# A graph-attention kernel of four layers on four streams: another order of the steps, and another agenda for their preparation

## The chip, the cores and the metric

The kernel runs on one core of a Trainium2 chip. The metric is the device time of one execution in microseconds (us). TensorE (PE in the profile) does matrix products and transposes, VectorE (DVE), ScalarE (ACT) and GpSimd (POOL) do elementwise work, SyncE (SP) starts the DMA transfers. Each engine has its own queue of instructions and waits for the others through semaphores.

## The reference, cut to what matters

There are 16 batch items of 1024 nodes with 256 features, one adjacency matrix for all, and four layers. Each layer normalises, clips at zero, and adds an attention layer to the residual `x`:

```python
h = jnp.maximum(_layernorm(x, axis=-1), 0.0)
x = x + _Ln_gnn_ref(h, adj, W, a)

# one attention layer (layers 0 and 2: four heads of 64; layers 1 and 3: one head of 256)
Wh = h @ W
e = leaky(e_src[:, None] + e_dst[None, :])        # 1024 x 1024 for each head
e = where(adj > 0, e, -big)
out = elu(softmax(e, axis=-1) @ Wh)               # relu in layer 3
```

The kernel does one layer of one item in a *step*; there are 16 x 4 = 64 steps, with four items ("streams") in flight. All is float32.

## The kernel before: the parts that the change touches

A step has three parts. Its **preparation**: statistics of `x`, normalisation, transposes, projection to `whx` (the projected features, with a column of weights), and the row factors `g`, which are sent through DRAM to all partitions. Its **weights and aggregation**: VectorE makes a tile `w` of 128 x 1024 attention weights for each head and each of eight column blocks, TensorE multiplies it with `whx`, ScalarE evicts the result to `y`. Its **finish**: divide by the sum of weights, ELU, add to `x`.

```python
# preparation (pieces in the order of the agenda)
def stats(half):            # 2 pieces; VectorE, four chunks each
    for c in range(half * HALF, (half + 1) * HALF):
        nc.vector.bn_stats(bn[:, c, :], xs[b][:, c, :])
    ...                     # after half 1: combine, ten small operations on GpSimd -> rstd, shift
def normalise(half):        # 2 pieces; ScalarE, four chunks each
        nc.scalar.activation(xn[:, q, :], xs[b][:, c, :], AF.Identity,
                             bias=st["shift"][:, c:c + 1], scale=st["rstd"][:, c:c + 1])
def transpose(half, k):     # TensorE, four transposes; then ScalarE evicts with Relu
def project(c):             # TensorE, two matmuls; then ScalarE (and GpSimd for four heads)
out = [stats(0), stats(1), normalise(0), normalise(1)]
for half in range(2):
    out += [transpose(half, 0), transpose(half, 1)]
    out += [project(c) for c in the half's four chunks]
out += [factors, rows, fetch_heads(n + 1), None]       # 20 pieces in all

# finish: (slot of the following step, piece)
def scaled(half):           # GpSimd: y times 1/sum; then min(y, 0)
def exponential(half):      # ScalarE
def add(half):
    nc.vector.scalar_tensor_tensor(e, e, -1.0, yh, op0=ALU.add, op1=ALU.max)
    nc.gpsimd.tensor_add(xh, xh, e)
return [(0, divide), (0, scaled(0)), (1, scaled(1)), (1, exponential(0)), (2, exponential(1)),
        (2, add(0)), (3, add(1))] + ...                # layer 3: another add, then store, load

# the main loop: every step has eight groups, "slots" k = 0..7
for n in range(len(steps)):
    for k, (h, i0, per) in enumerate(groups(n)):
        ...
        emit_tiles(place[n, h, C - 1] + 1, must=True)   # weights that this group needs
        aggregate(n, h, i0, per)                        # TensorE, then eviction on ScalarE
        if i0 + per == C:
            done["free"] = place[n, h, C - 1] + 1
        while ending and ending[0][0] <= k:             # finish of step n - 1
            ending.pop(0)[1]()
        ...
        prepare(8 * n + k)                              # pieces of the agenda that are due
        ahead = 6 if per > 1 else 3
        emit_tiles(min(done["tiles"] + ahead, done["free"] + WBUFS))   # weights ahead; WBUFS = 18
    ...
    ending = finish(n)
```

Everything is emitted in this order, and each engine does its instructions in the order of emission. Weights for a step are made ahead only once its preparation is complete by the agenda. A step with four heads has two groups for each head, with 64 aggregation matmuls of 64 output rows in each; a step with one head has eight groups of eight matmuls of 128 rows. (The profile counts each float32 matmul twice.)

The **agenda** says for each of the 20 pieces of step n's preparation in which slot it is emitted, counted in slots of the whole program from `8 * (n - 2)`. Before the change:

```python
AFTER_FOUR = (-3, -2, -1, 0, 1, 1, 2, 2, 3, 3, 4, 4, 5, 5, 6, 6, 7, 8, 8, 10)
SOON = (0, 0, 1, 2, 3, 3, 4, 4, 5, 5, 5, 5, 6, 6, 7, 7, 8, 9, 9, 11)
AFTER_ONE = (0, 1, 2, 3, 4, 4, 5, 5, 6, 6, 7, 7, 8, 8, 9, 9, 10, 11, 11, 13)
LATE = (0, 0, 1, 1, 2, 2, 3, 3, 3, 3, 3, 3, 4, 4, 4, 4, 5, 6, 6, 8)

for n, (b, l) in enumerate(steps):
    free = 8 * (last[b % STREAMS] + 1) + (8 if l == 0 else 5) if b % STREAMS in last else -99
    ...
    if free > start + kind[0]:          # the stream's step before isn't finished by then
        kind = LATE
        start = max(free, agenda_of[-1][0] + 5)
    agenda_of.append([start + k for k in kind] if n > 1 else ...)
```

`last` is the step in which the same stream was last worked on. In the order before, a stream's steps are four apart in most of the program (three to six at its ends), and the numbers of heads of the steps run 4 1 4 1 4 1 1 4 1 4 4 1 4 1 1 4 and so on: pairs of steps with four heads and pairs with one head occur.

Of the kernel before, what the change touches and what calls it, by code (L numbers as in the profile page):

```python
# [35 lines left out]
STREAMS = 4  # L36
# [2 lines left out]

AFTER_FOUR = (-3, -2, -1, 0, 1, 1, 2, 2, 3, 3, 4, 4, 5, 5, 6, 6, 7, 8, 8, 10)
SOON = (0, 0, 1, 2, 3, 3, 4, 4, 5, 5, 5, 5, 6, 6, 7, 7, 8, 9, 9, 11)
AFTER_ONE = (0, 1, 2, 3, 4, 4, 5, 5, 6, 6, 7, 7, 8, 8, 9, 9, 10, 11, 11, 13)
LATE = (0, 0, 1, 1, 2, 2, 3, 3, 3, 3, 3, 3, 4, 4, 4, 4, 5, 6, 6, 8)


LAYERS = [
    (4, 0.2, 0, 0),  # L50
    (1, 0.2, 0, 0),
    (4, 0.2, 128, 1),
    (1, 0.01, 0, 1),
]
# [3 lines left out]
def kernel(ctx: ExitStack, tc: tile.TileContext, x, adj, ws, avs, out):  # L58
# [38 lines left out]

    L = len(LAYERS)
    steps = order_of_steps(B, L)
    xs = {}  # L100
    state = [dict() for _ in steps]
# [337 lines left out]
    last, agenda_of = {}, []  # L439
    for n, (b, l) in enumerate(steps):  # L440

        free = 8 * (last[b % STREAMS] + 1) + (8 if l == 0 else 5) if b % STREAMS in last else -99
        last[b % STREAMS] = n
        start = 8 * (n - 2)
        before = [LAYERS[steps[max(n - i, 0)][1]][0] for i in (0, 1, 2)]
        if before[2] == 1:
            kind = SOON if before[:2] == [4, 1] else AFTER_ONE
        else:
            kind = SOON if l == 0 else AFTER_FOUR
        if free > start + kind[0]:  # L450
            kind = LATE
            start = max(free, agenda_of[-1][0] + 5)
        agenda_of.append([start + k for k in kind] if n > 1 else [-2] * 10 + [-1] * 10)
        if n > 2:

            was = agenda_of[n - 1]
            assert agenda_of[n][2] >= was[4] and agenda_of[n][3] >= was[10]
# [95 lines left out]
def order_of_steps(B, L):  # L553


    depth = B // STREAMS * L
    one = [[(k // L * STREAMS + s, k % L) for k in range(depth)] for s in range(STREAMS)]
    turns = [0, 1, 2, 0, 3, 2] + [0, 1, 2, 3] * (depth - 4) + [1, 0, 3, 2, 1, 0, 3, 2, 1, 3]
    return [one[s].pop(0) for s in turns]


# [22 lines left out]
```

## Time and profile before

| | before |
|---|---|
| median of 3 runs | 2699.22 us (2696.39 to 2703.35) |
| span of the profiled run | 2700.4 us |
| mean granted clock of TensorE | 0.984 |
| the chain that ended last, by engine | PE 82%, DVE 8%, ACT 4%, issue 3%, POOL 2%, DMA 1% |
| the chain, costliest lines | aggregation 61%, projection 17%, weight tiles 6%, transposes 4% |
| one weight tile on VectorE, 1280 of them | 1274 ns |
| DMA engines, mean rate over the span | 48 GB/s |

A line of instruction groups reads: line of the kernel, engine, operation, what is written and read, shapes, count, then the busy time in us with the mean of one in ns, then the idle time of that engine just before them with what ended it. A line of the timeline reads: start in us, length in us, engine, line, operation, tiles, shapes, count, and in brackets the engine's idle time before it and what released it. In a table of stretches each row gives the stretch, its length, the busy time of each engine with the number of instructions, the granted clock, the DMA share and GB/s.

### The profile page before, as it was taken

Reading aid. Unit: us, or ns where it says so; the run is one execution under the profiler, and the core shown is the slowest. Engines: PE = TensorE matmul, PEld = TensorE weight load, DVE = VectorE, ACT = ScalarE, POOL = GpSimd, SP = SyncE. Lnnn points to the kernel's source line nnn. Section 1 sums busy time; section 2 is a strip of 40 time slices with the busy share of each in tenths; the row PEclk is TensorE's granted clock in tenths of the full one; section 3 lists DMA queues with packets and bytes.
Section 4 is the critical chain, followed back from the end, with each engine's and each line's share of the span. In section 5 each row is a group of like instructions: output and inputs, shape, how many; then the busy total and the mean of one; then the engine's idle time right before and its main releaser. Section 6 shows DMA issues by size and latency. Waiting matters only on the chain.

```text
span 2700.4 us, 89532 instructions
## 1 busy us (share of the span) xinstructions
PE 2567.4 (95%) x40080; PEld 2271.1 (84%) x40080; DVE 1903.4 (70%) x2059; ACT 1228.1 (45%) x3338; POOL 987.8 (37%) x1234
## 2 busy tenths in 40 slices
PE   4899999999999999999999999999999999999998
PEld 3787888888888888888888888888888888788876
DVE  5796586477785688667875778748687567678742
ACT  4343445445444544554444554544435444444431
POOL 2143433532514434344242353452342443443321
PEclk8899999999999999999999999999999999999999
DMA  4211101112012111002211201101202110111011
GB/s 137 76 42 37 30 26 41 35 62 81 26 61 67 42 42 33 18 33 72 73 34 49 72 33 43 41 25 57 80 27 72 63 41 19 34 40 43 33 33 55
DMA packets 63694, 130.12 MB, mean 48 GB/s; under 512 B 6224, under 2 KB 41808, under 8 KB 63312
## 3 DMA queue, kind: packets, MB, share of 16 engines
q1 hardware_dynamic: 61984, 123.88, 13.7%
q8 instruction: 316, 5.18, 0.8%
q10 hardware_dynamic: 1328, 0.52, 0.1%
q14 instruction: 66, 0.54, 0.1%
HBM read 106.95 MB, written 17.43 MB: 46 GB/s over the span
## 4 chain that ended last, share of the span: by engine, by line
PE 82%; DVE 8%; ACT 4%; issue 3%; POOL 2%; DMA 1%; DVEq 0%; SPq 0%; ACTq 0%; POOLq 0%
PE acc L327 61%; PE pp L255 17%; DVE w L311 6%; PE pp L243 4%; DVE bn L205 1%; ACT xn L235 1%; DMA wx<-in_L_gnn_W 1%; POOL rstd L226 1%; ACT whx L257 1%; ACT g L306 0%; ACT e L361 0%; ACT whx L261 0%; PE pp L282 0%; ACT y L331 0%; POOL y L352 0%
## 5 line engine op out<-in xcount | busy, mean ns | idle before, releaser
L327 PE MATMUL acc<-whx,w 128*64 128x65 f32 x36864 | 1951.8, 242 | 41.3 <-DVE w L311 30.4
L327 PEld LDWEIGHTS acc<-whx,w 128*64 128x64 f32 x36864 | 1768.0, 146 | 223.5 <-issue 69.9
L311 DVE SCALAR_TENSOR_TENSOR w<-g,rcol,mask 128x1024 f32<-128x1024 f32 x1280 | 1544.1, 1274 | 440.5 <-ACT g L306 394.6
L331 ACT ACTIVATE y<-acc 128x260 f32<-128x260 f32 (+1 forms) x512 | 196.5, 384 | 1089.8 <-PE acc L327 1089.7
L255 PE MATMUL pp<-wx,hT 128*128 128x258 f32 (+1 forms) x2048 | 514.1, 394 | 5.7 <-ACT hT L244 3.2
L352 POOL TENSOR_TENSOR y<-y,r 128x1024 f32<-128x1024 f32 x128 | 242.3, 1897 | 618.0 <-DVE r L348 614.4
L255 PEld LDWEIGHTS pp<-wx,hT 128*128 128x128 f32 x2048 | 376.2, 191 | 75.1 <-ACT whx L261 6.0
L266 POOL TENSOR_TENSOR whx<-whx 128x256 f32<-128x256 f32 x256 | 160.0, 629 | 461.5 <-ACT whx L264 460.4
L368 POOL TENSOR_TENSOR x<-x,e 128x1024 f32<-128x1024 f32 x96 | 226.6, 2365 | 274.7 <-DVE e L367 250.1
L235 ACT ACTIVATE xn<-x,shift,rstd 128x256 f32<-128x256 f32 x512 | 264.2, 590 | 135.0 <-POOL shift L229 122.4
L367 DVE SCALAR_TENSOR_TENSOR e<-e,y 128x1024 f32<-128x1024 f32 x96 | 117.7, 1226 | 197.1 <-ACT e L361 197.1
L257 ACT ACTIVATE whx<-pp,nbias 128x4 f32<-128x4 f32 (+1 forms) x512 | 134.9, 264 | 166.4 <-PE pp L255 155.2
L243 PE MATMUL pp<-ident,xn 128*128 128x128 f32 x1024 | 158.7, 288 | 43.7 <-ACT xn L235 34.1
L205 DVE BATCH_NORM_STATS2 bn<-x 128x6 f32<-128x256 f32 x512 | 173.0, 407 | 28.5 <-DMA x<-in_x 25.8
L243 PEld LDWEIGHTS pp<-ident,xn 128*128 128x128 f32 x1024 | 117.1, 144 | 82.5 <-ACT xn L235 43.8
L306 ACT ACTIVATE g<-gs 128x1024 f32<-128x1024 f32 x160 | 162.4, 1018 | 8.4 <-DVE w L311 5.4
L244 ACT ACTIVATE hT<-pp 128x512 f32<-128x512 f32 x256 | 142.9, 592 | 26.6 <-PE pp L243 24.5
L261 ACT ACTIVATE whx<-pp,whx 128x256 f32<-128x256 f32 x256 | 121.4, 474 | 0.0
L220 POOL TENSOR_TENSOR dev<-bn 128x8 f32<-128x8 f32 x63 | 16.1, 256 | 276.5 <-DVE bn L205 276.5
L361 ACT ACTIVATE e<-e 128x1024 f32<-128x1024 f32 x96 | 100.8, 1050 | 30.0 <-POOL e L357 30.0
L226 POOL TENSOR_TENSOR rstd<-rstd,neghalf 128x8 f32<-128x8 f32 (+1 forms) x65 | 107.0, 1646 | 19.2 <-DVE shift L227 14.3
L357 POOL TENSOR_SCALAR e<-y 128x1024 f32<-128x1024 f32 x96 | 99.8, 1040 | 8.4
(58 smaller groups left out, 550.7 us busy)
## 6 DMA issues: line engine op xcount, KB each, us to landing
gs<-grow SPq DMA_DIRECT2D x160, 512.0 KB
out<-x SPq DMA_DIRECT2D x32, 512.0 KB
x<-in_x SPq DMA_DIRECT2D x15, 1024.0 KB
w<-in_adj SPq DMA_DIRECT2D x8, 512.0 KB
x<-in_x SPq DMA_DIRECT2D x2, 512.0 KB
wx<-in_L_gnn_W SPq DMA_DIRECT2D x3, 256.0 KB
e<-in_L_gnn_a SPq DMA_DIRECT2D x6, 128.0 KB
grow<-gT SPq DMA_DIRECT2D x32, 16.0 KB
```

The costliest lines, as they stand in the source:

```text
L205: nc.vector.bn_stats(bn[:, c, :], xs[b][:, c, :])
L235: nc.scalar.activation(xn[:, q, :], xs[b][:, c, :], AF.Identity, bias=st["shift"][:, c:c + 1], scale=st["rstd"][:, c:c + 1])
L243: nc.tensor.transpose(pt[:, q, :], st["xn", half][:, q, k * P:(k + 1) * P], ident)
L255: nc.tensor.matmul(pw, lhsT=st["hT", half][:, k, q * P:(q + 1) * P], rhs=wx[l][:, k, :], start=(k == 0), stop=(k == K - 1))
L257: nc.scalar.activation(whx[:, c, :, D], pw[:, F + H:F + 2 * H], AF.Exp, bias=nbias[l], scale=slope)
L266: nc.gpsimd.tensor_tensor(whx[:, c, :, 0:D], whx[:, c, :, 0:D], whx[:, c, :, D:D + 1].to_broadcast([P, H, D]), op=ALU.mult)
L306: nc.scalar.activation(g, state[n]["gs", h], AF.Copy)
L311: nc.vector.scalar_tensor_tensor(w, state[n]["g", h], state[n]["rcol"][:, jc, h:h + 1], masks[LAYERS[steps[n][1]][3]][:, jc, :], op0=ALU.m ...
L327: nc.tensor.matmul(acc[o % P:o % P + cols, q, :], lhsT=st["w", h, jc][:, o:o + cols], rhs=st["whx"][:, jc, h, :], start=(jc == 0), stop=(j ...
L331: nc.scalar.activation(st["y"][:, i0:i0 + per, h, :], acc, AF.Copy)
L352: nc.gpsimd.tensor_tensor(yh, yh, r[:, :, None].to_broadcast([P, HALF * H, D]), op=ALU.mult)
L368: nc.gpsimd.tensor_add(xh, xh, e)
```

## The change

The steps are put into another order, in which a step with four heads and a step with one head alternate strictly in all but the first and last few. A stream's step with one head then comes three steps after its last one, its step with four heads five after. The agenda follows: one list for steps with four heads (the former `AFTER_FOUR`), a new one for those with one head, and `SOON` only for the first steps. The earliest slot for a preparation after the finish of the stream's last step moves from 5 to 2. What is computed, the instructions and the buffers stay as they are. The aim is an even load: a step with four heads needs 32 weight tiles from VectorE, one with a single head 8, so that VectorE can make tiles for the first while the second is aggregated.

```diff
-AFTER_FOUR = (-3, -2, -1, 0, 1, 1, 2, 2, 3, 3, 4, 4, 5, 5, 6, 6, 7, 8, 8, 10)
+FOUR = (-3, -2, -1, 0, 1, 1, 2, 2, 3, 3, 4, 4, 5, 5, 6, 6, 7, 8, 8, 10)
+ONE = (2, 3, 4, 5, 5, 5, 6, 6, 7, 7, 7, 7, 8, 8, 8, 8, 9, 10, 10, 12)
 SOON = (0, 0, 1, 2, 3, 3, 4, 4, 5, 5, 5, 5, 6, 6, 7, 7, 8, 9, 9, 11)
-AFTER_ONE = (0, 1, 2, 3, 4, 4, 5, 5, 6, 6, 7, 7, 8, 8, 9, 9, 10, 11, 11, 13)
 LATE = (0, 0, 1, 1, 2, 2, 3, 3, 3, 3, 3, 3, 4, 4, 4, 4, 5, 6, 6, 8)
...
-        free = 8 * (last[b % STREAMS] + 1) + (8 if l == 0 else 5) if b % STREAMS in last else -99
+        free = 8 * (last[b % STREAMS] + 1) + (8 if l == 0 else 2) if b % STREAMS in last else -99
...
-        before = [LAYERS[steps[max(n - i, 0)][1]][0] for i in (0, 1, 2)]
-        if before[2] == 1:
-            kind = SOON if before[:2] == [4, 1] else AFTER_ONE
-        else:
-            kind = SOON if l == 0 else AFTER_FOUR
+        kind = ONE if LAYERS[l][0] == 1 else SOON if n < 4 else FOUR
...
     depth = B // STREAMS * L
     one = [[(k // L * STREAMS + s, k % L) for k in range(depth)] for s in range(STREAMS)]
-    turns = [0, 1, 2, 0, 3, 2] + [0, 1, 2, 3] * (depth - 4) + [1, 0, 3, 2, 1, 0, 3, 2, 1, 3]
+    turns = [0, 1, 2, 0, 3, 1, 2] + [0, 3, 1, 0, 2, 1, 3, 2] * (depth // 2 - 2)
+    turns += [0, 3, 1, 0, 2, 3, 1, 2, 3]
```

## The prediction

> **What bounds the kernel now.** I read the page first, then the groups by form, then stretches of the span cut at the ends of steps, then the timeline around one step. I call a step of a layer with four heads a *four-step*, one with a single head a *one-step*, and the eight parts into which the schedule cuts every step its *slots* 0 to 7.
>
> The page's busy line and its slices:
>
> ```profile
> PE 2567.4 (95%) x40080; PEld 2271.1 (84%) x40080; DVE 1903.4 (70%) x2059; ACT 1228.1 (45%) x3338; POOL 987.8 (37%) x1234
> ...
> PE   4899999999999999999999999999999999999998
> ```
>
> TensorE is busy 95% of the span and short of that only at the ends. The table of stretches says how much is left to win (columns: us, then busy us of PE, PEld, DVE, ACT, POOL, then the granted clock):
>
> ```profile
> 74.00:480.30 406.30, 377.39 (x6980) 336.59 (x6977) 310.80 (x342) 177.14 (x472) 143.06 (x182) 0.96 0.13 42
> 480.30:2208.20 1727.90, 1695.83 (x26420) 1506.96 (x26420) 1242.07 (x1323) 813.24 (x2226) 659.40 (x814) 1.00 0.15 49
> 2208.20:2700.00 491.80, 462.22 (x6514) 403.17 (x6513) 314.91 (x328) 203.11 (x551) 167.32 (x196) 0.98 0.12 38
> ```
>
> In the 43 steps of the middle stretch TensorE is idle 1727.9 - 1695.8 = 32 us, at the two ends 29 and 30 us. Step by step (cut at the last eviction of each) the middle idle lies in four-steps, above all where two of them are neighbours: one-steps last 32.5 to 35.7 us with next to no idle time, four-steps alone 44.4 to 48 us with 0.1 to 2.3 us, and the second of a pair looks like this:
>
> ```profile
> 1319.80:1366.40 46.60, 42.10 (x1053) 38.30 (x1048) 44.48 (x45) 18.27 (x47) 17.69 (x22) 0.96 0.05 14
> ```
>
> There VectorE is busy 44.5 of 46.6 us and TensorE waits for it. That is what strict alternation is meant to cure.
>
> [...] here the residual add takes 2.36 us on GpSimd and the two-input step before it 1.23 us on VectorE. [...] after the idle of 4.43 us shown below, the stretch
>
> ```profile
> 2328.20:2331.40 3.20, 3.03 (x30) 2.41 (x32) 1.94 (x4) 3.20 (x8) 2.43 (x6) 0.50 0.00 0
> ```
>
> has a granted clock of 0.50.
>
> **The change, part by part.** No instruction is added or removed; all durations of single instructions stay. Three things move.
>
> *Order.* I wrote out both sequences. Before, a stream's steps are mostly four apart and pairs of four-steps and of one-steps occur twice in 16 steps. After, from step 7 to 59, every four-step is followed by a one-step; a four-step comes five after its stream's last, a one-step only three. For 25 of the one-steps (numbers 10 to 58) the picture is the same: its predecessor is four-step M-1, its preparation falls into one-step M and the next four-step, and it runs as M+2.
>
> *Gain.* With no pairs, TensorE's idle time in the middle should nearly vanish: of the 32 us I count 25. [...] seconds of pairs have a mean clock of 0.96, so 0.04 x 46 = 1.8 us each for five of them, 9 us. For the ends I count 20 of the 59 us: the old order has seven steps there that come three after their predecessor, some with long waits; what the new order has of that kind is counted below. And some 9 us from smaller gaps on the weight-load side, which is my guess. Sum: -63 us.
>
> *Cost.* In M the finish of M-1 and the preparation of M+2 now meet. The finish adds the halves of the residual in slots 2 and 3; the new agenda puts the statistics of half 0 in slot 2, of half 1 in slot 3, right behind them, the normalisation of half 0 in slot 4 and its transposes on TensorE in slot 5. (The release moved from 5 to 2 allows it; before it was the statistics in slot 5 at the earliest.) What these steps take in a one-step after a four-step can be read in the kernel before, from step 54, which began at 2295. It is the timeline, with lines of other work left out:
>
> ```profile
> 2303.46 1.23 DVE L367 SCALAR_TENSOR_TENSOR e<-e,y 128x1024 f32<-128x1024 f32 x1 [6.93 <-ACT e L361]
> 2304.77 2.35 POOL L368 TENSOR_TENSOR x<-x,e 128x1024 f32<-128x1024 f32 x1 [2.14 <-DVE e L367]
> ...
> 2307.86 3.67 DVE L311 SCALAR_TENSOR_TENSOR w<-g,rcol,mask 128x1024 f32<-128x1024 f32 x3 [3.17 <-ACT g L306]
> ...
> 2311.44 1.22 DVE L367 SCALAR_TENSOR_TENSOR e<-e,y 128x1024 f32<-128x1024 f32 x1
> ...
> 2312.73 2.35 POOL L368 TENSOR_TENSOR x<-x,e 128x1024 f32<-128x1024 f32 x1 [5.62 <-DVE e L367]
> 2316.02 0.39 ACT L331 ACTIVATE y<-acc 128x257 f32<-128x257 f32 x1 [3.09 <-PE acc L327]
> ...
> 2322.51 0.21 POOL L220 TENSOR_TENSOR dev<-bn 128x8 f32<-128x8 f32 x1 [7.42 <-DVE bn L205]
> ...
> 2326.72 4.04 ACT L235 ACTIVATE xn<-x,shift,rstd 128x256 f32<-128x256 f32 x8 [6.84 <-POOL shift L229]
> ...
> 2327.37 0.33 PE L243 MATMUL pp<-ident,xn 128*128 128x128 f32 x1 [4.43 <-ACT xn L235]
> ```
>
> Now put the changed preparation into these times. The first add on GpSimd ends at 2304.77 + 2.35 = 2307.1. VectorE, waiting for it, makes four statistics (0.34 each, as 1.40 for four elsewhere in this timeline): 2308.5. The three weight tiles of slot 2 (3.67; their row factors are there by 2307.8): 2312.2. The second exponential step (1.22): 2313.4. The second add (2.35, and 0.1 of handover): 2315.9. Four statistics: 2317.3. The ten small GpSimd operations, here 2322.51 to 2326.72, 4.2 us: 2321.5. The first of the normalised blocks (0.6): 2322.2. TensorE meanwhile: slot 5's aggregation ends where its eviction begins, at 2316.0, and the transposes are next in its queue. So it stands idle 2322.2 - 2316.0 = 6.2 us. Then the transposes follow at the pace of the normalisation: in step 54 they took 2327.37 to 2330.10, 2.7 us, against 1.1 for eight undisturbed ones (1.09 in other parts of the trace): 1.6 us. Then the half clock. Step 3 of the kernel before shows it whole:
>
> ```profile
> 256.96 2.80 PE L243 MATMUL pp<-ident,xn 128*128 128x128 f32 x8 [5.66 <-ACT xn L235]
> 259.69 5.48 PE L327 MATMUL acc<-whx,w 128*64 128x65 f32 x128
> ```
>
> A group of 128 of these takes 3.95 us elsewhere, so 1.5 us more; [...] I count 1.3. Sum for one step: 6.2 + 1.6 + 1.3 = 9.1 us, nothing of it beside other TensorE work, since TensorE is what was full. Times 25: 228 us. The four projections that slot 0 of the next four-step now takes in one go cost little: 16 matmuls in a row took 4.01 us before, as much as two times eight at 2.01; I count 0.3 each, 7 us for 25.
>
> *Sum.* 2700 - 63 + 228 + 7 = 2872 us, said as 2870.
>
> **The rivals.** (1) *The alternation wins clean.* VectorE has its idle time in one-steps (10 to 20 of 34 us), the schedule seems made for them, and a statistic that waits there costs VectorE nothing. Then the gain of 63 us is all: about 2637 us. Against it speaks that not VectorE's time but the length of a chain counts: from the first exponential step to the first transpose 18.7 us are needed (2303.46 to 2322.2), and TensorE's slot 5 is over 12.5 us after that start (2316.0). (2) *Half of it.* If the three weight tiles don't get between the two exponential steps, because their row factors come late or in another order, the chain is 3.7 us shorter: 2.5 us idle, 1.6 of pace, and no half clock[...]: 4.1 x 25 = 103 us, so 2700 - 63 + 103 + 7 = 2747 us. For it: in some steps of before the two stand next to each other. Against it: the agenda marks the four-step's preparation as complete in slot 2, ahead of the tiles there. (3) *VectorE becomes the bound of the four-steps.* It needs some 30 tiles of 1.274 us (the mean of the weight group) plus two exponential steps of 1.2, 41 us, against TensorE's 45: close, but the ten tiles that the buffers allow ahead are made in the one-step. If it fails, 2 us per pair, 50 us more: 2920.
>
> **Range and chances.** Rival 2 and mixtures with the main case give the lower part, rival 3 and longer half clocks the upper: 2770 to 2925 us. The cost of a stall would have to fall below (63 - 7)/25 = 2.2 us for a faster kernel at all, and to nothing for more than 2% (below 2645): 0.05. Within 2% (up to 2753) means (2753 - 2700 + 56)/25 = 4.4 us at most: 0.07, as rival 2 lies just there. Slower: 0.88.
>
> **What would show it.** Right: TensorE's transposes with idle time before them of some 6 us, 25 times, released by the normalisation; ScalarE's normalisation released by GpSimd's shift; one-steps of some 43 us where before they were 34, four-steps at 45 to 46 without VectorE filling them; TensorE's busy share down to about 90% and a granted clock near 0.96. Wrong: transposes that wait under 1 us; or four-steps that grow instead; or, if the chain is there but short, the second exponential step directly behind the first half's statistics.

## The result, and the profile after

The changed kernel takes 2911.39 us (median of 4 runs, 2911.21 to 2912.41) against 2699.3 us before: a ratio of 1.0785, 95% interval 1.0767 to 1.0804. It is slower by 212 us; 2870 us were predicted, with a range of 2770 to 2925.

The page of the changed kernel, the busy line, the slices of TensorE and of its clock:

```profile
PE 2640.7 (91%) x40080; PEld 2292.7 (79%) x40080; DVE 1907.4 (66%) x2059; ACT 1232.6 (42%) x3338; POOL 975.5 (34%) x1234
...
PE   4889999999999999999999999999999999999988
...
PEclk8999999999999999999999999999999999999999
```

The busy share of TensorE fell by four points, and the slices still show nines: a loss of some 8% in short pieces hides in slices of 73 us. The table of stretches, cut at the ends of steps 8 and 58 (steps are counted from 0; after the busy times the granted clock), shows where it lies:

```profile
0.00:483.50 483.50, 401.77 (x6221) 348.38 (x6222) 328.88 (x400) 204.75 (x540) 164.18 (x234) 0.93 0.16 54
483.50:2700.00 2216.50, 2056.11 (x31298) 1784.47 (x31298) 1460.16 (x1543) 960.57 (x2622) 764.70 (x950) 0.96 0.13 43
2700.00:2909.60 209.60, 182.83 (x2570) 159.90 (x2566) 118.35 (x118) 67.30 (x177) 46.67 (x50) 0.93 0.12 39
```

The kernel before, cut at the ends of the same steps, in the same view:

```profile
0.00:480.30 480.30, 409.33 (x7148) 360.97 (x7149) 346.42 (x411) 211.77 (x563) 161.05 (x224) 0.95 0.17 55
480.30:2507.60 2027.30, 1981.84 (x31252) 1758.71 (x31252) 1461.53 (x1553) 951.14 (x2602) 780.13 (x960) 0.99 0.14 47
2507.60:2700.40 192.80, 176.21 (x1683) 151.43 (x1681) 95.44 (x98) 65.21 (x175) 46.59 (x50) 0.96 0.12 42
```

The middle grew by 2216.5 - 2027.3 = 189 us: TensorE's idle time from 45 to 160 us, its busy time by 74 us with the same matmuls, at a mean clock of 0.96 in place of 0.99. The start grew by 3 us, the end by 209.6 - 192.8 = 17 us. (The ends don't hold the same work, as the counts of matmuls show: the new order has five four-steps among its first nine steps and two among its last five, the old one six and one.) What the middle's idle time waits for (the view of waits, for TensorE in this stretch; us in total, times, longest):

```profile
PE pp L242 <- ACT xn L234: 146.2, 24, 6.1
```

The transposes wait for the normalisation, once in each pair of steps. One of these, in the timeline of the changed kernel, a one-step that began at 1154:

```profile
1162.30 1.22 DVE L366 SCALAR_TENSOR_TENSOR e<-e,y 128x1024 f32<-128x1024 f32 x1 [7.84 <-ACT e L360]
1163.61 2.35 POOL L367 TENSOR_TENSOR x<-x,e 128x1024 f32<-128x1024 f32 x1 [3.05 <-DVE e L366]
...
1165.99 1.40 DVE L204 BATCH_NORM_STATS2 bn<-x 128x6 f32<-128x256 f32 x4 [2.47 <-POOL x L367]
1167.31 3.65 DVE L310 SCALAR_TENSOR_TENSOR w<-g,rcol,mask 128x1024 f32<-128x1024 f32 x3
...
1170.88 1.21 DVE L366 SCALAR_TENSOR_TENSOR e<-e,y 128x1024 f32<-128x1024 f32 x1
...
1172.17 2.35 POOL L367 TENSOR_TENSOR x<-x,e 128x1024 f32<-128x1024 f32 x1 [6.21 <-DVE e L366]
1174.55 1.41 DVE L204 BATCH_NORM_STATS2 bn<-x 128x6 f32<-128x256 f32 x4 [2.46 <-POOL x L367]
...
1180.26 2.07 ACT L234 ACTIVATE xn<-x,shift,rstd 128x256 f32<-128x256 f32 x4 [8.49 <-POOL shift L228]
1180.91 2.80 PE L242 MATMUL pp<-ident,xn 128*128 128x128 f32 x8 [6.09 <-ACT xn L234]
...
1183.50 4.78 PE L326 MATMUL acc<-whx,w 128*128 128x257 f32 x16
```

Read it from below: TensorE is idle 6.09 us until the normalisation's first block; that waited 8.49 us on ScalarE for GpSimd; GpSimd began when the second statistics ended at 1176; these waited for the second add, this for the second exponential step, and that stood on VectorE behind three weight tiles and the first statistics. The last line is a group of 16 that takes 3.64 us elsewhere: half clock. The stretches around it, with the clock as the third number from the end, 0.50 in the second and the third row:

```profile
1174.90:1179.00 4.10, 0.00 (x0) 0.00 (x0) 4.10 (x7) 0.00 (x0) 2.49 (x7) 1.00 0.00 2
1179.00:1182.40 3.40, 1.44 (x4) 0.57 (x4) 3.40 (x4) 2.15 (x5) 1.05 (x4) 0.50 0.01 2
1182.40:1185.80 3.40, 3.40 (x11) 2.94 (x12) 3.40 (x7) 3.12 (x7) 0.00 (x0) 0.50 0.02 5
1185.90:1190.00 4.10, 4.10 (x20) 3.56 (x20) 1.01 (x4) 1.16 (x4) 2.53 (x7) 1.00 0.00 0
```

From the first exponential step to the first transpose it is 18.61 us; predicted were 18.7.

A pair of steps (mean over steps 8 to 55, cut at the last eviction) went from 47.0 + 34.3 to 48.7 + 40.1 us.

### The profile page after: what moved, and what is told of

Same layout as the page of the kernel before. It is cut to its first block, busy times and chain, and to the rows that moved or that the text cites. A ratio compares the mean times of both kernels' runs of the same rounds, so it can differ in the third digit from the quotient of the medians.

```text
span 2909.6 us, 89557 instructions
## 1 busy us (share of the span) xinstructions
PE 2640.7 (91%) x40080; PEld 2292.7 (79%) x40080; DVE 1907.4 (66%) x2059; ACT 1232.6 (42%) x3338; POOL 975.5 (34%) x1234
## 4 chain that ended last, share of the span: by engine, by line
PE 72%; DVE 9%; POOL 9%; ACT 4%; issue 3%; DMA 2%; DVEq 0%; SPq 0%; ACTq 0%; POOLq 0%
PE acc L326 50%; PE pp L254 16%; PE pp L242 6%; DVE w L310 5%; POOL x L367 5%; DVE e L366 2%; POOL rstd L225 2%; DVE bn L204 2%; ACT e L360 1%; ACT xn L234 1%; DMA gs<-grow 1%; DMA wx<-in_L_gnn_W 1%; ACT whx L260 1%; ACT y L330 0%; DMA grow<-gT 0%
## 5 line engine op out<-in xcount | busy, mean ns | idle before, releaser
L254 PE MATMUL pp<-wx,hT 128*128 128x264 f32 (+1 forms) x2048 | 515.1, 393 | 9.3 <-ACT gT L283 7.8
L265 POOL TENSOR_TENSOR whx<-whx 128x256 f32<-128x256 f32 x256 | 179.3, 707 | 717.6 <-ACT whx L263 717.6
L242 PE MATMUL pp<-ident,xn 128*128 128x128 f32 x1024 | 201.9, 325 | 203.4 <-ACT xn L234 194.5
L242 PEld LDWEIGHTS pp<-ident,xn 128*128 128x128 f32 x1024 | 130.3, 158 | 269.2 <-ACT xn L234 236.7
L204 DVE BATCH_NORM_STATS2 bn<-x 128x6 f32<-128x256 f32 x512 | 178.9, 412 | 163.8 <-POOL x L367 138.0
L347 DVE RECIPROCAL r<-y 128x8 f32<-128x8 f32 (+1 forms) x64 | 17.5, 273 | 156.5 <-ACT y L330 156.5
```

Source lines behind the costliest of these rows:

```text
L242: nc.tensor.transpose(pt[:, q, :], st["xn", half][:, q, k * P:(k + 1) * P], ident)
L254: nc.tensor.matmul(pw, lhsT=st["hT", half][:, k, q * P:(q + 1) * P], rhs=wx[l][:, k, :], start=(k == 0), stop=(k == K - 1))
L265: nc.gpsimd.tensor_tensor(whx[:, c, :, 0:D], whx[:, c, :, 0:D], whx[:, c, :, D:D + 1].to_broadcast([P, H, D]), op=ALU.mult)
```

## The experiments

My theory: alternation is sound, and the loss is the chain from finish to transposes, which has three slots too few and is made of queue places as much as of data. Rivals: the alternation itself costs (VectorE, buffers, crowded four-steps); the distance of three is too short whatever the lists; the residual add on GpSimd alone sets the time. Pairs are means as above, and all ratios are to the kernel before, measured along on the same chip.

| run | median us | ratio (95% interval) | four-step + one-step, us | clock |
|---|---|---|---|---|
| the changed kernel | 2911.4 | 1.0785 (1.0767 to 1.0804) | 48.7 + 40.1 | 0.955 |
| one-steps' list later | 2913.3 | 1.0785 (1.0767 to 1.0803) | 60.5 + 28.5 | 0.957 |
| tiles behind | 2811.2 | 1.0407 (1.0390 to 1.0424) | 48.8 + 36.4 | 0.968 |
| adds together | 2832.6 | 1.0488 (1.0474 to 1.0503) | 48.7 + 37.2 | 0.968 |
| tiles behind, adds together | 2728.5 | 1.0101 (1.0086 to 1.0117) | 48.7 + 33.4 | 0.985 |
| new order, old agenda | 2837.5 | 1.0505 (1.0489 to 1.0521) | 51.0 + 35.7 | 0.967 |
| both lists later | 2652.8 | 0.9816 (0.9801 to 0.9830) | 49.6 + 29.9 | 0.988 |
| one slot more, with tiles and adds | 2674.4 | 0.9898 (0.9885 to 0.9912) | 51.0 + 29.0 | 0.987 |
| kernel before, adds together | 2699.6 | 0.9993 (0.9984 to 1.0001) | | 0.986 |
| both lists later, adds together | 2647.6 | 0.9803 (0.9790 to 0.9817) | 49.5 + 29.9 | 0.990 |

### The one-steps' list later

```diff
-ONE = (2, 3, 4, 5, 5, 5, 6, 6, 7, 7, 7, 7, 8, 8, 8, 8, 9, 10, 10, 12)
+ONE = (2, 3, 6, 7, 7, 7, 8, 8, 8, 8, 8, 8, 9, 9, 9, 9, 10, 11, 11, 12)
```

> The new order with only the one-steps' list moved: normalisation from slots 4 and 5 to 6 and 7, first transposes from 5 to 7, the rest one slot later. Theory (the chain from the finish to the transposes is too long for slot 5, and nothing else is wrong with the order): the normalised block is there 26.8 us after the step's begin, slot 7's group ends at 27.8 us, so the idle 6.1 us, the slow pace and the half clock go: 25 x 9.3 = 232 us less, some 10 us more at the start, about 2670 us; one-steps near 32 us. Rival (alternation itself costs, by VectorE or by the buffers for weights): the time moves from the one-steps into the four-steps, and the kernel stays above 2850 us.

2913.3 us: no gain, as the rival said, with four-steps of 60.5 us. But the reason isn't the rival's. The one-step's stall is gone (28.5 us, next to no idle time), and a new one stands in the four-step. Its timeline:

```profile
1188.94 3.95 PE L326 MATMUL acc<-whx,w 128*64 128x65 f32 x128
...
1191.37 1.39 DVE L204 BATCH_NORM_STATS2 bn<-x 128x6 f32<-128x256 f32 x4
...
1197.05 2.07 ACT L234 ACTIVATE xn<-x,shift,rstd 128x256 f32<-128x256 f32 x4 [5.66 <-POOL shift L228]
...
1199.98 0.37 ACT L330 ACTIVATE y<-acc 128x260 f32<-128x260 f32 x1
...
1200.52 0.47 ACT L260 ACTIVATE whx<-pp,whx 128x256 f32<-128x256 f32 x1
...
1201.05 3.81 PE L254 MATMUL pp<-wx,hT 128*128 128x258 f32 x8 [6.22 <-ACT whx L260]
```

ScalarE stands 5.66 us before the normalisation of the *next four-step*, which slot 7 issues while its statistics are late on VectorE. The evictions of finished matmuls queue up behind it (the one at 1199.98 is for the matmuls in the first line, which had ended by 1192.9), and TensorE, with its two buffers in PSUM full, waits 6.22 us for the eviction of a projection. In the changed kernel the same statistics are as late, but TensorE is late as well: by slot 7 they are ready (GpSimd's last operation on them ends at 1191.2 in its pair above), and this normalisation, at 1197.29, doesn't wait.

### Both lists later

```diff
-FOUR = (-3, -2, -1, 0, 1, 1, 2, 2, 3, 3, 4, 4, 5, 5, 6, 6, 7, 8, 8, 10)
+FOUR = (-3, -2, 0, 1, 2, 2, 3, 3, 4, 4, 5, 5, 6, 6, 7, 7, 8, 9, 9, 11)
+ONE = ...                                              # as in the run before
```

> As the run with the one-steps' list later, and the four-steps' list from the first normalisation on one slot later too, its last entry 11. In that run ScalarE stood 5.7 us in each pair before the normalisation of the next four-step (issued in slot 7, its statistics were late), and the evictions of the projections queued behind it: TensorE waited 6.2 us there. Theory (one queue's waiting instruction moves the stall, and the alternation itself costs nothing): with that normalisation out of slot 7 the four-steps fall from 60.5 to some 52 us while one-steps stay at 28.5: 25 x 8.3 us less than 2913, about 2700 us, a bit under with the start. Rival (16 projections and the transposes crowded into a four-step are too much for the two buffers in PSUM): four-steps stay above 58 us, kernel above 2850 us.

2652.8 us, faster than the kernel before by 1.8%, and 47 us better than I expected: I had counted the second stall at 8.3 us for each pair; it was 89.0 - 79.5 = 9.5 us, and the start gained too. In the view of stretches, a one-step, a four-step, and the 50 steps of the middle:

```profile
1219.30:1249.20 29.90, 29.90 (x142) 25.95 (x142) 15.41 (x23) 10.96 (x28) 15.28 (x18) 1.00 0.20 71
1249.20:1298.50 49.30, 49.08 (x1112) 43.63 (x1111) 42.80 (x40) 26.41 (x78) 10.95 (x18) 1.00 0.19 57
454.80:2448.50 1993.70, 1984.47 (x31290) 1748.42 (x31288) 1461.35 (x1552) 963.45 (x2627) 747.27 (x958) 1.00 0.15 48
```

TensorE is idle 9 us in 1994, at full clock. The wait for the eviction of a projection, in the middle of the run before and of this one:

```profile
PE pp L254 <- ACT whx L260: 155.7, 27, 6.2
...
PE pp L254 <- ACT whx L260: 0.2, 1, 0.2
```

The list moves more than that one normalisation, the three weight tiles too (its last entry); what the normalisation alone is worth was not run. The alternation with its distances of three and five therefore costs nothing by itself; with this agenda it needs 2027.3 - 1993.7 = 34 us less in the middle than the old order with its own. Whether later lists would have helped the old order too was not tried, so not all of the 34 us need be the order's.

### Tiles behind; adds together; both

The first takes only the three weight tiles out of the chain; the second only puts the second half's exponential step and add ahead of the first half's statistics.

```diff
-FOUR = (-3, -2, -1, 0, ..., 7, 8, 8, 10)
+FOUR = (-3, -2, -1, 0, ..., 7, 8, 8, 11)               # tiles behind
...
-                (2, lambda: add(0)), (3, lambda: add(1))] + (
+                (2, lambda: add(0)), (2, lambda: add(1))] + (    # adds together
```

> The changed kernel with the last entry of the four-steps' list 11 in place of 10, so that the three weight tiles of slot 2 come behind the second half's statistics. Theory: the chain is shorter by their 3.65 us, so TensorE's idle time before the transposes falls from 6.1 to 2.5 us; [...] the half clock (6.8 us in each pair of steps) goes as well; some 5.5 us for each of 25 pairs, about 2770 us, mean clock near 0.98. If the residual add on GpSimd alone sets the time, idle stays near 6 us and the kernel near 2910 us. If half clock comes from any gap, the clock stays near 0.955 and the time is about 2810 us.

> The changed kernel with the second half's add in slot 2, and the three tiles left where they are, between the two halves' statistics. Theory (the chain adds up instruction by instruction on VectorE and GpSimd): the second exponential step comes right behind the first, the first half's statistics 1.2 us later, then the tiles (3.7), then the second half's statistics, done some 2.3 us earlier than in the changed kernel: idle 3.9 us in place of 6.1, and still a half clock in most pairs; 25 x 2.6 us less, about 2845 us. Rival (the two moves are independent, the gain of 83 us between the runs two and three is that of the adds): about 2828 us. If the add on GpSimd is all that counts, idle falls by less than 1 us and the time stays above 2890 us.

> As the run with the tiles behind, and the second half's add also in slot 2, ahead of the first half's statistics. Theory: second add done 2.4 us earlier relative to that run less what GpSimd is still busy with, statistics done 17 us after the step's begin, first normalised block at 21.7 us against a slot 5 that ends at 20.7: 1 us idle, 2.1 us in all for each pair in place of 9.3, about 2730 us. Rival: no change against the run before it, as the first half's add was not what statistics waited for.

Tiles behind: idle time 2.5 us as expected, but 2811 us, the figure I had given for a half clock that comes from any gap. The timeline of TensorE in one such pair, and the stretch after it with its clock:

```profile
711.74 0.33 PE L242 MATMUL pp<-ident,xn 128*128 128x128 f32 x1 [2.53 <-ACT xn L234]
712.23 0.33 PE L242 MATMUL pp<-ident,xn 128*128 128x128 f32 x1 [0.16 <-ACT xn L234]
...
713.21 1.33 PE L242 MATMUL pp<-ident,xn 128*128 128x128 f32 x5 [0.16 <-ACT xn L234]
714.34 4.65 PE L326 MATMUL acc<-whx,w 128*128 128x257 f32 x16
```

```profile
713.10:716.30 3.20, 3.09 (x10) 2.72 (x11) 3.20 (x6) 3.20 (x8) 0.00 (x0) 0.50 0.34 128
```

After 2.53 us of idle time and a few single transposes this stretch has a clock of 0.50; 23 of the 24 pairs of the middle had half clock, and the mean clock of the run is 0.968. Adds together: idle 3.4 us (expected 3.9) and 2832.6 us, nearer to the rival's 2828 than to my 2845. Both together: idle 1.06 us, half clock in 3 of the 24 pairs, a mean clock of 0.985, 2728.5 us (expected 2730). The two moves gain 100 and 79 us alone and 183 together. That the sum fits so well is partly chance: of the idle time they take 3.6 and 2.7 us alone but 5.0 together, a little less than the sum, and only together do they take most of the half clock with it (mean clock 0.968 with either alone, 0.985 with both). The add on GpSimd alone doesn't set the time: the tiles have nothing to do with it and were worth 100 us.

### One slot more

```diff
+ONE = (2, 3, 5, 6, 6, 6, 7, 7, 7, 7, 8, 8, 8, 8, 8, 8, 9, 10, 10, 12)
+FOUR = (-3, -2, 0, 1, 1, 1, 2, 2, 3, 3, 4, 4, 5, 5, 6, 6, 7, 8, 8, 11)
...                                                     # and adds together
```

> As the run with both adds in slot 2 and the tiles behind, and one slot more between chain and transposes: the one-steps' normalisation in slots 5 and 6, first transposes in slot 6, and the four-steps' normalisation in slots 0 and 1 in place of 7 and 0. Theory: the normalised block is there 22.2 us after the step's begin, slot 6's group ends at 24.7 us, so the last 1.2 us idle and 1.1 us of pace go: 25 x 2.2 us less than 2728, about 2675 us, faster than the kernel before by 0.9%, with a clock of 0.99. Rival (what is left is the order's own cost): 2720 us or more.

2674.4 us (expected 2675): what was left was the chain's last 2 us. TensorE's transposes now wait for the normalisation only once in the whole run.

### The order alone, and the kernel before with the adds together

The first keeps the lists, the rules and the release of the kernel before, and takes only the new `turns`. The second changes the finish of the kernel before as above.

> The new order of steps alone, with the agenda of the kernel before (its lists and its release at slot 5). By its rules 25 or so one-steps then take the late list: statistics in slot 5, transposes in slot 7. Theory: each shows the stall that the kernel before shows in its few late steps (4.4 us idle, 1.6 us of pace, about 1.5 us of half clock, 7.5 us), 24 x 7.5 in place of 25 x 9.3: about 2865 us. Rival (the new lists are to blame, not the distance of three): near 2670 us.

> The kernel before, its order and agenda, with the second half's add also in slot 2. It tells whether the gain of this move belongs to the new order or is to be had in both. Theory: the kernel before has room of three slots and more between finish and statistics in all but its seven late steps, so only these gain, at most 2 us each: 2685 to 2700 us. Rival: a gain of over 2% as in the new order.

The new order with the old agenda takes 2837.5 us, 28 us less than expected: the late list shows its stall as in the kernel before, but in the middle the idle time ranges from 2.3 to 4.5 us rather than being always 4.4. So neither the old nor the new lists suit the distance of three. The kernel before with the adds together is unchanged, within 0.2%: there the time doesn't hang on that chain.

### Both lists later, adds together

> As the run with both lists later, and the second half's add in slot 2. Theory: there TensorE no longer waits for the chain, so a shorter chain is worth nothing in the middle; at the start and the end a few us: 2645 to 2653 us. Rival: 2620 us or less, if the chain still costs something that the idle time doesn't show.

2647.6 us, the best of all: 2.0% faster than the kernel before (ratio 0.9803, 0.9790 to 0.9817). The gain over the run without the adds is small, as expected, and lies at the ends; in the middle the pairs are alike.

## Why the prediction was right, and where it was off

*The chain.* "it stands idle 2322.2 - 2316.0 = 6.2 us": measured 6.09 in the pair shown, and 146.2 us over 24 waits. The order on VectorE (exponential step, statistics, three tiles, exponential step, statistics) came out as worked out. The experiments confirm the terms: the tiles' 3.7 us shorten the idle time from 6.1 to 2.5 us.

*Pace and half clock.* 1.6 + 1.3 us were predicted. The transposes took 2.80 us against 1.1, 1.7 more; the group behind them 4.78 against 3.64, 1.1 more (over the 24 pairs of the middle 1.0 to 1.8, in the mean 1.3). The sum is right. That it would be 1.3 us and not the 1.5 of step 3 was an estimate of mine. In the trace half clock lasts 6.83 us at each of the 24 stalls of the middle; in the pair shown 1.9 us of these, from 1179.0 to 1180.9, fall into the idle time itself.

*Steps.* Four-steps at "45 to 46" and one-steps at "some 43" came out at 48.7 and 40.1: of the 16 pieces of projection in a pair, 13.3 lie in the four-step on average, where 11.1 did before, more than I had counted. The pair, 88.8 us, is what the sum says.

*The middle as a whole.* 228 + 7 less 43 of the gain is 192 us; measured were 189. The sum is closer than its parts: only 24 of the 25 stalls lie between the ends of steps 8 and 58; the first is in step 8. If the run with both lists later stands for the same order without them, they cost 2216.5 - 1993.7 = 223 us, 9.3 for each, against 9.1 + 0.3: the cost was right. The order's gain in these steps was then 34 us at most, not 43. (The 43 come from a cut at other steps, so this split is rough.)

*The ends: here the sum failed.* "For the ends I count 20 of the 59 us": they did not gain 20 us but lost 3 + 17, and these 40 us are about the whole distance between 2870 and 2911 (9 of them are the stall in step 8, which the sum held, and the smaller gain in the middle makes up for these). As a four-step has moved from the start to the end, and is some 13 us longer than a one-step, the start lost about 16 us like for like and the end about 4. The view of waits for the start and the end, first the changed kernel, then the kernel before:

```profile
PE pp L242 <- ACT xn L234: 35.4, 7, 9.1
PE pp L242 <- ACT xn L234: 12.8, 6, 8.5
...
PE pp L243 <- ACT xn L235: 18.2, 4, 9.4
PE pp L243 <- ACT xn L235: 3.2, 1, 3.2
```

What failed is the count of the steps that wait: "what the new order has of that kind is counted below", but only steps 10 to 58 are counted there. Steps 62 and 63 come three after theirs as well, and in step 60 TensorE waits 8.5 us for the normalisation of step 62. At the start I had taken only one-steps *three* after their predecessor for late. Steps 5, 6 and 8 come four after theirs, so their residual was ready long before; their transposes waited all the same, 4.3, 4.1 and 3.7 us. The changed kernel's timeline for step 5, within step 3:

```profile
240.21 1.22 DVE L366 SCALAR_TENSOR_TENSOR e<-e,y 128x1024 f32<-128x1024 f32 x1
...
241.34 1.40 DVE L204 BATCH_NORM_STATS2 bn<-x 128x6 f32<-128x256 f32 x4
...
249.00 2.80 PE L242 MATMUL pp<-ident,xn 128*128 128x128 f32 x8 [4.25 <-ACT xn L234]
```

The second half's statistics follow the exponential step of *another* stream at once, with no wait for an add between: queue place alone delays them, and TensorE waits 4.25 us. With the tiles behind, this wait and that of step 8 fall to 0.2 us, while that of step 6 stays at 4.1 us.

*Rivals.* Rival 1, a clean alternation at 2637 us, is nearly reached once the lists fit and the adds are together: 2647.6 us. Rival 2's idle time of 2.5 us was shown by the run with the tiles behind, but its "no half clock", which no trace had shown, was wrong: 23 of the 24 pairs of the middle had it, at a mean clock of 0.968 over the run. Rival 3, a VectorE that bounds the four-steps, was not seen: in the two fastest runs VectorE is idle some 7 us in each four-step (49.3 - 42.8 = 6.5 in the one shown).

## What to carry to other kernels

In a schedule of in-order queues, measure a chain's length against the time of the slots that it is given, counting what stands *ahead in each queue*, not only what the data need; here both sides could be read to 0.1 us from one step of the old trace. When a stall is removed and the time doesn't move, look for the next instruction that waits at the head of a shared queue: a normalisation issued too early stood 5.66 us on ScalarE and held up evictions that were ready, and TensorE waited 6.22 us. An order and its agenda must be judged together: this order was 7.9% slower with one agenda and 1.8% faster with another.

## What had not been expected of the hardware

Half clock came after shorter idle stretches than I had expected. Rival 2, and the theory for the run with the tiles behind, expected none after 2.5 us of idle time, which no trace had shown. With the tiles behind, 2.5 us of idle time and some 2 us of single transposes were followed by 3.4 or 6.8 us of half clock in 23 of the 24 pairs of the middle (mean clock of the run 0.968); with both moves, 1.06 us of idle time in 3 of 24 (0.985). What decides in which pair it comes is not shown by any run. In the middle of the kernel before, the trace has seven half-clock stretches of 3.41 us; in the middle of the changed kernel 24 of 6.83 us, one for each stall, beginning 88.75 us apart.
